# Cross-attention on one core: where two attention products of batch 30 and the first sums for x of batch 1 stand

## The chip, the cores and the metric

The kernel runs on one core of one Trainium2 chip. The core has TensorE (PE: matrix products out of SBUF into PSUM; PEld is its weight load), VectorE (DVE), ScalarE (ACT), GpSimd (POOL) and SyncE (SP, which only issues transfers here). GpSimd issues transfers too, and only those that add what they carry to what lies at their target. The metric is the time of one execution on the device in microseconds (us), median of three runs.

## What is computed

For each of 32 batches, x and y (the context) are 256 x 1024, f32. `w_qk`, `w_v` and `w_t` are 256 x 256.

```python
x_q = jnp.einsum('oc,bcn->bno', w_qk, y)
x_k = jnp.einsum('oc,bcn->bon', w_qk, x)
x_v = jnp.einsum('oc,bcn->bon', w_v, x) + b_v[None, :, None]
energy = jnp.einsum('bnc,bcm->bnm', x_q, x_k)
attention = jax.nn.softmax(energy, axis=-1)
attention = attention / (1e-07 + attention.sum(axis=1, keepdims=True))
x_r = jnp.einsum('bcn,bnm->bcm', x_v, attention)
x_r = jax.nn.relu(jnp.einsum('oc,bcn->bon', w_t, x - x_r) + b_t[None, :, None])
return x + x_r
```

The softmax runs along the rows; then each column is divided by its sum S over the rows. S needs the whole matrix of a batch, so nothing of the last product of a batch can start on the attention before S is there.

## The kernel before

**Seven products.** All is f32. Each large product is done as a 2 x 2 block product with seven block products instead of eight (Strassen's scheme in Winograd's form). They are called P1 to P7 here. The class `Seven` (L245) has what all four kinds share: three banks of PSUM, `one`, `two` and `three`; P1, P6, P7 and P4 follow one another in `one`, P5 and P3 in `two`, P2 in `three`. Between them ScalarE copies `one` after P1 (p1s), `two` after P5 (p5s) and `one` after P6 (w) into SBUF. VectorE makes a result block from one bank and one copy: c11 from P2 and p1s, c12 from P3 and w, c22 from P7 and p5s; c21 is P4's bank itself. P4 may only start in `one` when c22 has read it.

**The four kinds, per batch b.** `Keys` (pg) multiplies x by w_qk's square, result gx. `Values` (pu) makes ut from x, with w_t and w_v taken together. `Energy` (pe) makes the energies; a batch is cut into four tiles t = 0 to 3, called E0 to E3, each of which gives 128 rows of both halves of e; ScalarE takes the exp, and VectorE adds each row block, divided by its row sum, into `acc` (`share`, the "acc" rows). `Attention` (po) makes the output. `columns` (L543) reduces acc to `part`, `inverse` (L551) has a small product pS and turns it into rc, the inverse column sums, laid over all partitions.

**Attention.** A product has one call on x (`xpart`, L461, the x-call) and four on e (`epart`, L466, the e-calls, one for each block of 128 rows); a call is two MATMUL records[...]. `begin` issues the x-calls of P1, P5 and P2, which need no S. `run` (L505) has VectorE scale e by the row and column factors (`normal`, four instructions of 128x512 each time) and make t1 to t4 (`mix`, two instructions each): t1, t2 and t4 lie in a tile `et`, t3 in place of e's block b12 (L445). P1 needs normal(0,0), P2 normal(1,0), P5 t1, P6 t2, P3 b22, P7 t3, P4 t4. TensorE's order there is P1, P2, P5, P6's and P3's x-calls, half of P3's e-calls, P6, the rest of P3, P7. `combine` (L485) is two instructions on VectorE, the difference z and then relu plus x (L489), followed by the store. `end` (P4) and `c21` (relu on ScalarE, plus x on VectorE, the store) of batch b stand in batch b + 1, after P1 and P5 of its E0 (L612). In the last batch they stand at the very end.

**What overlaps S.** While VectorE and ScalarE finish E3 and S, TensorE has Keys and Values of the next batch to do. In the last batch there is no next one: after E3's P4 it has only `begin` (L682), then pS and then the attention of that batch.

**Sums.** The seven-product scheme needs sums of the blocks of each operand. For Values' result ut they are `us`, four subtractions on GpSimd (L365), in a pool with one buffer; us is read by P3, P5, P6 and P7 of the attention. For x and y of later batches (`summed`, L218) SyncE loads blocks into xs (ys), and three adding transfers by GpSimd, each of which needs the one before to have landed, complete them: `steps` at L238. For x these are `xsteps`, called at the ends of the tiles t = 1 to 3 (L647). Keys of the next batch needs xs: P5 the first of them, P6 the second, P4 the third. ut gets its bias by another such transfer, `u.bias()`, from uc.

**Order.** TensorE, VectorE, ScalarE and GpSimd each run their instructions in the order of the program text (`InOrder`, L66, ties each to the one before), so the text is the schedule of each engine; the recorded line of all of them is L77, and one goes by the names of tiles. Transfers by SyncE are in order on its queue. Waits between engines, and the choice of the buffer in a pool, are made by the framework. The pool `up` (x's sums, ut) and the pool `cp` of temporaries (p1s, p5s, w, z) have two buffers for each name, `one` and `et` one, PSUM eight banks.

Before the first batch, the text has Keys for batch 0, gt (the sums of Keys' result, L582), Values for batch 0 and `u.bias()`; E0 to E3 follow.

Of the kernel before, what the change touches and what calls it, by code (L numbers as in the profile page):

```python
# [9 lines left out]
F32 = mybir.dt.float32  # L10
AF = mybir.ActivationFunctionType
ALU = mybir.AluOpType
# [4 lines left out]
def kernel(  # L17
# [29 lines left out]
    nc = tc.nc  # L47
    B, C, N = x.shape
    P = 128
    KC = C // P  # L50
    NT = N // P
    MB = 512
    MH = N // MB
    HT = NT // 2
# [27 lines left out]
    pe, dve, act, pool = (InOrder(g) for g in (nc.tensor, nc.vector, nc.scalar, nc.gpsimd))  # L82
# [4 lines left out]
    loaded = {}  # L87

    def load(tag, b, pieces=1):
        from_, p = (x, xp) if tag == "x" else (y, yp)  # L90
        to = p.tile([P, KC, N], F32, tag=tag, name=f"{tag}_{b}")
        from_ = from_[b].rearrange("(k p) n -> p k n", p=P)
        W = KC // pieces
        for j in range(pieces):
            nc.sync.dma_start(to[:, ts(j, W)], from_[:, ts(j, W)])
        loaded[tag, b] = to
# [28 lines left out]
    bt = const.tile([P, KC, 1], F32, name="bt")  # L125
# [81 lines left out]
    up = ctx.enter_context(tc.tile_pool(name="up", bufs=2))  # L207
    one = ctx.enter_context(tc.tile_pool(name="one", bufs=1))
# [3 lines left out]
    def temp(tag, name):  # L212
        return cp.tile([P, MB], F32, tag=tag, name=name)
# [117 lines left out]
    class Values(Seven):  # L331
# [32 lines left out]

        def factors(self):  # L365

            us = one.tile([P, 4, HT, P], F32, tag="us", name=f"us_{self.b}")
            s1, s2, s3, s4 = (us[:, j] for j in range(4))
            a11, a12, a21, a22 = (self.block(i, h) for i in range(2) for h in range(2))
            steps = [  # L370
                lambda: pool.tensor_tensor(s1, a21, a22, ALU.add),
                lambda: pool.tensor_tensor(s2, s1, a11, ALU.subtract),
                lambda: pool.tensor_tensor(s3, a11, a21, ALU.subtract),
                lambda: pool.tensor_tensor(s4, a12, s2, ALU.subtract),
            ]
            return (a11, a12, s4, a22, s1, s2, s3), steps
# [58 lines left out]
    class Attention(Seven):  # L435


        def __init__(self, b, xr, ur):
            super().__init__("o", b)
            self.xr, self.ur = xr, ur  # L440
            et = ep.tile([P, 3, HT, MB], F32, tag="et", name=f"et_{b}")
            self.b11, self.b12 = e[:, :HT, ts(0, MB)], e[:, :HT, ts(1, MB)]
            self.b21, self.b22 = e[:, HT:, ts(0, MB)], e[:, HT:, ts(1, MB)]
            self.t1, self.t2, self.t4 = (et[:, j] for j in range(3))
            self.t3 = self.b12  # L445
            self.er = self.b11, self.b21, self.b22, self.t4, self.t1, self.t2, self.t3

        def normal(self, half, h):
# [14 lines left out]
                into, t_left[j - 1], self.xr[j - 1], start=not onto, stop=False, skip_group_check=True  # L463
            )

        def epart(self, into, j, tiles=range(HT)):  # L466
            for t in tiles:
                pe.matmul(
                    into,
                    self.ur[j - 1][:, t],  # L470
                    self.er[j - 1][:, t],
                    start=False,
                    stop=(t == HT - 1),
                    skip_group_check=True,
                )
# [9 lines left out]
        def combine(self, i, h, in0, in1, op):  # L485
            z = temp("z", f"z_{self.b}_{i}_{h}")
            dve.tensor_tensor(z, in0, in1, op)
            xt = loaded["x", self.b]
            dve.scalar_tensor_tensor(z, z, 0.0, xt[:, i, ts(h, MB)], ALU.max, ALU.add)  # L489
            self.store(i, h, z)  # L490
# [11 lines left out]
            self.xpart(self.two, 5)  # L502
            self.xpart(self.three, 2)

        def run(self, u):  # L505

            self.normal(0, 0)
            if u:
                u.c22()
            self.normal(1, 0)  # L510
            self.normal(0, 1)
            self.mix(self.t1, self.b11, self.b12, ALU.add)
            self.normal(1, 1)
            self.mix(self.t2, self.t1, self.b22, ALU.subtract)
            self.epart(self.one, 1)
            self.p1s = self.biased(self.one, "p1s", bt[:, 0, :])
            self.epart(self.three, 2)
            self.epart(self.two, 5)
            self.p5s = self.biased(self.two, "p5s", bt[:, 1, :])
            self.xpart(self.one, 6, True)  # L520
            if u:
                u.p4()
                u.c21()
                u.c11()
                u.c12()
            self.c11()
            self.xpart(self.two, 3, True)
            self.epart(self.two, 3, range(HT // 2))
            self.epart(self.one, 6)
            self.w = self.biased(self.one, "w", nbt[:, 0, :])  # L530
            self.mix(self.t3, self.b12, self.b22, ALU.subtract)
            self.mix(self.t4, self.b21, self.t2, ALU.subtract)
            self.epart(self.two, 3, range(HT // 2, HT))
            self.c12()
            self.xpart(self.one, 7, True)
            self.epart(self.one, 7)
            self.c22()

        def end(self):
            self.xpart(self.one, 4, True)  # L540
            self.epart(self.one, 4)

    def columns(b):  # L543

# [20 lines left out]
    xr, _ = summed("x", 0)  # L565
# [15 lines left out]
    lhs, gsteps = g.factors()  # L581
    for step in gsteps:  # L582
        step()
    u = Values(0, xr)
    u.p1()
    u.p5()
# [7 lines left out]
    u.p4()  # L594
    u.c21()
    u.bias()

    before = None
    for b in range(B):
        more = b + 1 < B  # L600
        pair = []

        for t in range(HT):
            now = Energy(b, t, lhs, rhs)
            pair.append(now)
            now.p1()
            if t > 0:
                pair[t - 1].exp(1)
            now.p5()
            if t == 0:  # L610
                if before is not None:
                    before.end()  # L612
                    before.c21()
                    if more:
                        load("x", b + 1)
                e = ep.tile([P, NT, N], F32, tag="e", name=f"e_{b}")
                acc = one.tile([P, N], F32, tag="acc", name=f"acc_{b}")
                ur, usteps = u.factors()
            if t > 1:
                pair[t - 2].share(0)  # L620
            if t == 0:
                now.p6()
            now.p2()
            now.c11()
            if t == 1:
                pair[0].scale(1)
            if t > 1:
                pair[t - 1].share(1)
            if t > 0:
                now.p6()  # L630
            if t == 1:
                act.activation(acc, e[:, HT, :], AF.Copy, scale=scales[HT])
            if t > 0:
                pair[t - 1].p4()
                pair[t - 1].c21()
                pair[t - 1].exp(0)
            now.p3()
            now.c12()
            now.p7()
            now.c22()  # L640
            if t == 0:
                for step in usteps:
                    step()
                if more:
                    xn, xsteps = summed("x", b + 1)
            elif more:
                xsteps[t - 1]()  # L647
        last = pair[-1]

        if more:  # L650
            g = Keys(b + 1, xn)
            g.p1()
        last.exp(1)
        if more:
            g.p5()
        pair[2].share(0)
        last.p4()
        last.c21()
        last.share(1)
        if more:  # L660
            load("y", b + 1)
            rhs, ysteps = summed("y", b + 1)
            g.p6()
        last.exp(0)
        if more:
            g.p2()
            g.c11()
            g.p3()
        last.share(0)
        part = columns(b)  # L670
        if more:
            g.p7()
            g.c12()
            g.c22()
            un = Values(b + 1, xn)
            un.p1()
            un.p5()
            un.p2()
            un.p6()
        else:  # L680
            now = Attention(b, xr, ur)
            now.begin()  # L682
        rc = inverse(b, part)
        if more:
            un.p3()
            g.p4()
            g.c21()
            un.p7()
            lhs, gsteps = g.factors()

        if more:
            now = Attention(b, xr, ur)
            now.begin()
            ysteps[0]()
            now.run(un)
            ysteps[1]()
            un.bias()
            for step in gsteps:
                step()
            ysteps[2]()  # L700
            before = now
            xr, u = xn, un
        else:
            now.run(None)
            now.end()
            now.c21()


# [28 lines left out]
```

## Time and profile before

| | us |
|---|---|
| median of 3 runs (2168.8 to 2169.19) | 2169.16 |
| the profiled execution | 2169.38 |
| its span, from first to last instruction | 2167.6 |
| TensorE busy | 2147.3 |
| VectorE busy | 1806.0 |
| ScalarE busy | 787.7 |
| GpSimd busy | 597.3 |
| mean granted clock of TensorE | 0.997 |

A row of the timeline has the start in us from the span's start, the busy time, the engine, the line, the operation, what is written from what, the shapes and the number of instructions merged; in brackets the idle time before it and what ended that. "SPq", "POOLq" are the issue of transfers. A row of the list of waits has who waited for whom: us in total, times, longest. A group's or a merged row's busy time holds overlapping records: MATMULs of 128x512 are recorded with 0.59 us each but start 0.43 us apart. What counts for the time is idle time of TensorE, which is busy for 99% of the span; batches start 66.56 us apart.

### The profile page before, as it was taken

Reading aid. Unit: us, or ns where it says so; the run is one execution under the profiler, and the core shown is the slowest. Engines: PE = TensorE matmul, PEld = TensorE weight load, DVE = VectorE, ACT = ScalarE, POOL = GpSimd, SP = SyncE. Lnnn points to the kernel's source line nnn. Section 1 sums busy time; section 2 is a strip of 40 time slices with the busy share of each in tenths; the row PEclk is TensorE's granted clock in tenths of the full one; section 3 lists DMA queues with packets and bytes.
Section 4 is the critical chain, followed back from the end, with each engine's and each line's share of the span. In section 5 each row is a group of like instructions: output and inputs, shape, how many; then the busy total and the mean of one; then the engine's idle time right before and its main releaser. Section 6 shows DMA issues by size and latency. Waiting matters only on the chain.

```text
span 2167.6 us, 19880 instructions
## 1 busy us (share of the span) xinstructions
PE 2147.3 (99%) x6366; PEld 1064.3 (49%) x6366; DVE 1806.0 (83%) x2963; ACT 787.7 (36%) x1321; POOL 597.3 (28%) x488
## 2 busy tenths in 40 slices
PE   9999999999999999999999999999999999999997
PEld 4455545554455545455544555444554545555453
DVE  5798888988888988889888888888898888988887
ACT  4134432344422444323443324443234433344421
POOL 4322323222233222332232322223322323223220
PEclk9999999999999999999999999999999999999999
DMA  5555666556655566565566554665555666556630
GB/s 142 123 121 140 146 130 146 114 125 155 153 124 126 120 148 146 122 144 115 135 150 140 133 124 122 149 154 121 132 118 143 146 128 149 111 128 155 144 75 20
DMA packets 139049, 282.60 MB, mean 130 GB/s; under 512 B 9152, under 2 KB 42688, under 8 KB 138944
## 3 DMA queue, kind: packets, MB, share of 16 engines
q0 software_dynamic: 75936, 114.83, 33.8%
q1 hardware_dynamic: 62464, 166.48, 23.0%
q8 instruction: 51, 0.84, 0.2%
q14 instruction: 54, 0.44, 0.1%
q10 hardware_dynamic: 544, 0.00, 0.0%
HBM read 181.67 MB, written 33.55 MB: 99 GB/s over the span
## 4 chain that ended last, share of the span: by engine, by line
PE 98%; DMA 1%; DVE 1%; issue 0%; POOL 0%; ACT 0%; DVEq 0%
PE po L77 44%; PE pe L77 34%; PE pu L77 9%; PE pg L77 9%; DMA xs<-xs 0%; DMA ut<-uc 0%; DMA xs<-in_x_dram 0%; PE idle L142 0%; DVE acc L77 0%; PE pS L77 0%; POOL us L77 0%; DVE e L77 0%; PE pw L184 0%; PE pg L169 0%; DVE z L77 0%
## 5 line engine op out<-in xcount | busy, mean ns | idle before, releaser
L77 PE MATMUL pe<-gt,ys 128*128 128x512 f32 x768 | 392.3, 592 | 0.0
L77 DVE SCALAR_TENSOR_TENSOR e<-e,ri,rc 128x512 f32<-128x512 f32 x512 | 348.4, 743 | 1.1
L77 DVE SCALAR_TENSOR_TENSOR acc<-e,ri,acc 128x1024 f32<-128x1024 f32 x224 | 289.0, 1290 | 8.0
L77 PE MATMUL pe<-gx,y 128*128 128x512 f32 x512 | 261.5, 592 | 0.0
L77 PEld LDWEIGHTS pe<-gt,ys 128*128 128x128 f32 x768 | 145.8, 190 | 184.1 <-issue 183.0
L77 PE MATMUL po<-e,us 128*128 128x512 f32 x512 | 235.4, 592 | 0.0
L77 PE MATMUL po<-e,ut 128*128 128x512 f32 x512 | 227.7, 598 | 2.7 <-DVE e L77 2.7
L77 PE MATMUL po<-et,us 128*128 128x512 f32 x512 | 230.2, 592 | 0.0
L77 POOL TENSOR_TENSOR gt<-gx 128x512 f32<-128x512 f32 x64 | 101.8, 1590 | 415.6 <-DVE gx L77 415.6
L77 ACT COPY ep1s<-pe 128x512 f32<-128x512 f32 x128 | 74.9, 585 | 306.1 <-PE pe L77 289.4
L77 ACT ACTIVATE e<-e,nm 128x1024 f32<-128x1024 f32 x128 | 147.1, 1149 | 99.1 <-DVE nm L77 97.6
L77 DVE TENSOR_TENSOR e<-e 128x1024 f32<-128x1024 f32 x64 | 178.9, 2833 | 0.0
L77 PEld LDWEIGHTS po<-e,ut 128*128 128x128 f32 x512 | 98.2, 192 | 126.5 <-issue 97.3
L77 PEld LDWEIGHTS po<-e,us 128*128 128x128 f32 x512 | 97.3, 190 | 122.4 <-issue 114.8
L77 PEld LDWEIGHTS pe<-gx,y 128*128 128x128 f32 x512 | 97.2, 190 | 121.9 <-issue 114.1
L77 PEld LDWEIGHTS po<-et,us 128*128 128x128 f32 x512 | 95.7, 190 | 124.1 <-issue 123.8
L77 DVE CUSTOM_DVE_ANT_0 e<-pe,ep1s 128x512 f32<-128x512 f32 x128 | 88.5, 691 | 79.6 <-ACT e L77 64.1
L77 DVE TENSOR_TENSOR z<-z,x 128x512 f32<-128x512 f32 x32 | 22.1, 692 | 153.9 <-ACT z L77 153.9
L77 ACT ACTIVATE e<-e,bias 128x1024 f32<-128x1024 f32 x128 | 147.4, 1152 | 0.5 <-DVE ri L77 0.5
L77 POOL DMA_DIRECT2D ut<-uc x32 | 50.7, 1584 | 313.1 <-DVE ut L77 257.2
L77 PE MATMUL pe<-gx,ys 128*128 128x512 f32 x256 | 130.9, 593 | 1.2 <-DVE nm L77 1.0
L77 PE MATMUL pe<-gt,y 128*128 128x512 f32 x256 | 130.7, 592 | 0.0
(113 smaller groups left out, 3360.9 us busy)
## 6 DMA issues: line engine op xcount, KB each, us to landing
y<-in_ctx_dram SPq DMA_DIRECT2D x32, 1024.0 KB, 4.9
ut<-uc POOLq DMA_DIRECT2D x32, 1024.0 KB, 9.7
out_dram<-z SPq DMA_DIRECT2D x128, 256.0 KB, 2.1
x<-in_x_dram SPq DMA_DIRECT2D x31, 1024.0 KB, 6.3
xs<-in_x_dram SPq DMA_DIRECT2D x62, 512.0 KB, 4.7
ys<-in_ctx_dram SPq DMA_DIRECT2D x62, 512.0 KB, 4.2
xs<-in_x_dram POOLq DMA_DIRECT2D x31, 512.0 KB, 9.2
xs<-xs POOLq DMA_DIRECT2D x31, 512.0 KB, 5.0
```

Source lines behind the costliest of these rows:

```text
L77: self.last = getattr(self.engine, name)(*args, **kwargs)
```

## The change

Six things are changed.

1. `us` comes from the pool with two buffers.
2. t3 goes into t1's place in `et` instead of e's block b12, so that P7 reads no part of e.
3. `combine` is split: `put` has the relu, the addition of x and the store. In all batches but the last two, P7, c22 and its `put` follow right behind `run`, where they stood at its end; c12 is in `run` for all but the last batch.
4. Of batch 30, P7 and P4 are left out where they stood, and take place in batch 31: P7's x-call before E3's P4, its e-calls behind E3's P4 and before `begin`, c22 behind `columns`, P4 behind pS; `put` and c21 stand in `run`, behind normal(1,0).
5. The end of the last batch is a function of its own, `finish`: P7 stands before the last e-call of P3, c22 before c12, and P4 with its relu, addition and store goes in two halves of 256 columns.
6. The sums for x of batch 1: the tile, its loads and the first adding transfer stand before Values of batch 0, the second and third behind `u.bias()`, and so ahead of the four us subtractions on GpSimd.

```diff
-            us = one.tile([P, 4, HT, P], F32, tag="us", name=f"us_{self.b}")
+            us = up.tile([P, 4, HT, P], F32, tag="us", name=f"us_{self.b}")
...
-            self.t3 = self.b12
+            self.t3 = self.t1
...
     def combine(self, i, h, in0, in1, op):
             z = temp("z", f"z_{self.b}_{i}_{h}")
             dve.tensor_tensor(z, in0, in1, op)
+            self.left = i, h, z
+
+        def put(self):
+            i, h, z = self.left
             xt = loaded["x", self.b]
             dve.scalar_tensor_tensor(z, z, 0.0, xt[:, i, ts(h, MB)], ALU.max, ALU.add)
             self.store(i, h, z)
...
-        def run(self, u):
+        def run(self, u, before=None):
...
             self.normal(1, 0)
+            if before:
+                before.put()
+                before.c21()
             self.normal(0, 1)
...
             self.c11()
+            self.put()
             self.xpart(self.two, 3, True)
-            self.epart(self.two, 3, range(HT // 2))
+            self.epart(self.two, 3, (0, 1))
             self.epart(self.one, 6)
...
-            self.epart(self.two, 3, range(HT // 2, HT))
-            self.c12()
-            self.xpart(self.one, 7, True)
-            self.epart(self.one, 7)
-            self.c22()
+            self.epart(self.two, 3, (2,))
+            if u:
+                self.epart(self.two, 3, (3,))
+                self.c12()
+                self.put()
...
+        def finish(self):
+            self.xpart(self.one, 7, True)
+            self.epart(self.one, 7)
+            self.epart(self.two, 3, (3,))
+            self.c22()
+            self.put()
+            self.c12()
+            self.put()
+            self.xpart(self.one, 4, True)
+            z = temp("z", f"z_{self.b}_1_0")
+            for cols in (ts(0, MB // 2), ts(1, MB // 2)):
+                self.epart(self.one, 4, cols=cols)
+                act.activation(
+                    z[:, cols], self.one[:, cols], AF.Relu, bias=bt[:, 1, :], scale=1.0
+                )
+                dve.tensor_tensor(
+                    z[:, cols], z[:, cols], loaded["x", self.b][:, 1, cols], ALU.add
+                )
+                nc.sync.dma_start(out[self.b, ts(1, P), cols], z[:, cols])
...
     for step in gsteps:
         step()
+    xn, xsteps = summed("x", 1)
+    xsteps[0]()
     u = Values(0, xr)
...
     u.bias()
+    xsteps[1]()
+    xsteps[2]()
...
             if t == 0:
-                if before is not None:
+                if before is not None and more:
                     before.end()
                     before.c21()
-                    if more:
-                        load("x", b + 1)
+                    load("x", b + 1)
...
-                if more:
+                if more and b > 0:
                     xn, xsteps = summed("x", b + 1)
-            elif more:
+            elif more and b > 0:
                 xsteps[t - 1]()
...
         last.exp(1)
         if more:
             g.p5()
+        else:
+            before.xpart(before.one, 7, True)
         pair[2].share(0)
         last.p4()
...
+        else:
+            before.epart(before.one, 7)
         last.exp(0)
...
+        else:
+            now = Attention(b, xr, ur)
+            now.begin()
         last.share(0)
         part = columns(b)
...
         else:
-            now = Attention(b, xr, ur)
-            now.begin()
+            before.c22()
         rc = inverse(b, part)
...
             now.run(un)
+            if b + 2 < B:
+                now.xpart(now.one, 7, True)
+                now.epart(now.one, 7)
+                now.c22()
+                now.put()
...
         else:
-            now.run(None)
-            now.end()
-            now.c21()
+            before.end()
+            now.run(None, before)
+            now.finish()
```

More of the change, by code (lines that the diff above doesn't have):

```diff
@@ L464, in xpart, with epart @@
             )
-        def epart(self, into, j, tiles=range(HT)):
+        def epart(self, into, j, tiles=range(HT), cols=slice(0, MB)):
             for t in tiles:
                 pe.matmul(
-                    into,
+                    into[:, cols],
                     self.ur[j - 1][:, t],
-                    self.er[j - 1][:, t],
+                    self.er[j - 1][:, t, cols],
                     start=False,
```

## The prediction

> **What bounds the kernel now.** I read the page's busy times first, then the list of waits for TensorE, then the timeline and the windows around each wait. The page:
>
> ```profile
> PE 2147.3 (99%) x6366; PEld 1064.3 (49%) x6366; DVE 1806.0 (83%) x2963; ACT 787.7 (36%) x1321; POOL 597.3 (28%) x488
> ```
>
> TensorE is the bound: only 20 us of the span are not busy. The list of waits says where its idle time is:
>
> ```profile
> PE pg L77 <- DMA xs<-xs: 5.7, 1, 5.7
> PE po L77 <- DVE e L77: 2.7, 1, 2.7
> PE pS L77 <- DVE part L77: 2.7, 1, 2.7
> ```
>
> Each occurs once in 32 batches, so the steady loop (66.56 us a batch in the chain of waits) has nothing to give. The 5.7 is in batch 0, the two 2.7 in batch 31. The timeline of batch 0:
>
> ```profile
> 26.87 1.72 POOL L77 DMA_DIRECT2D ut<-uc  x1 [4.47 <-ACT ut L77]
> ...
> 42.06 1.19 POOL L77 DMA_DIRECT2D xs<-in_x_dram  x1
> 48.21 1.20 POOL L77 DMA_DIRECT2D xs<-xs  x1 [4.95 <-DMA xs<-in_x_dram]
> ...
> 51.21 1.13 PE L77 MATMUL pe<-gx,ys 128*128 128x512 f32 x2
> ...
> 58.01 2.05 PE L77 MATMUL pg<-xs,gs 128*128 128x512 f32 x2 [5.68 <-DMA xs<-xs]
> 59.85 1.75 PE L77 MATMUL pg<-x,g 128*128 128x512 f32 x2
> 61.44 1.02 PE L77 MATMUL pg<-x,gs 128*128 128x512 f32 x2
> ```
>
> GpSimd stands idle from 22.41 to 26.87, then until 35.98 for ut's bias to land, makes the four us and only then starts x's sums for batch 1; the second lands at 57.87 where Keys' sixth product wants it at 52.17. A matmul call is two MATMULs, 0.857 us from start to start; the first two after the wait take 1.84 and 1.59. The windows (columns: us, busy PE, PEld, DVE, ACT, POOL, then granted clock) say why, and show the same in batch 31:
>
> ```profile
> 58.00:60.00 2.00, 1.99 (x3) 0.97 (x4) 0.00 (x0) 0.00 (x0) 0.92 (x1) 0.50 0.71 222
> 2129.80:2136.60 6.80, 5.36 (x7) 2.27 (x8) 6.76 (x11) 0.00 (x0) 0.00 (x0) 0.50 0.00 0
> ```
>
> The timeline of that place in batch 31:
>
> ```profile
> 2121.71 1.12 PE L77 MATMUL pe<-gx,ys 128*128 128x512 f32 x2 [1.05 <-DVE nm L77]
> ...
> 2128.09 0.41 PE L77 MATMUL pS<-part,fold 128*128 128x32 f32 x2 [2.68 <-DVE part L77]
> ...
> 2131.24 9.79 PE L77 MATMUL po<-e,ut 128*128 128x512 f32 x16 [2.74 <-DVE e L77]
> ```
>
> Idle for 1.05, 2.68 and 2.74 us, then at half clock until 2136.6.
>
> **The head.** Three transfers by GpSimd move. The first sum is issued right after gt, at 22.5 instead of 42.06; its loads by SyncE landed at 17.39 and keep their place. With 5.9 us as now it lands at 28.4. The bias keeps its issue at 26.87, as it waits for ut. The second sum waits for the first and the bias' issue (28.59): issued at 28.7, with its worst duration now (9.7) it lands at 38.4; were it to run wholly behind the bias (9.0), at 47. Needed at 52.17: hidden either way. The third (4.3 us) follows by 43 to 51, needed near 60. The us subtractions are now behind the third sum's issue: 40 to 45, at worst 48 to 53; their reader is attention of batch 0, after 64. So the wait of 58.01 - 52.17 = 5.84 goes, and with it the half clock: four MATMULs took 3.43 instead of 1.71, another 1.72. Sum 7.56.
>
> What is late next is VectorE. A us subtraction beside an acc sum costs it 1.1 us:
>
> ```profile
> 40.83 2.38 DVE L77 SCALAR_TENSOR_TENSOR acc<-e,ri,acc 128x1024 f32<-128x1024 f32 x1
> ```
>
> (the usual acc is 1.29). In batch 1, TensorE's last energy product has 0.5 us to spare for VectorE, in batch 0 it waits 0.29 (50.92 to 51.21). I take one such collision again, since us stays in that stretch; VectorE's lag then costs a further 0.2 at attention's fifth product, which has 0.25 to spare in batch 1. None would give +0.3, two -1.1. **Head: -7.35 (-6.2 to -7.85).**
>
> Here a rule weighs against the change: the Trainium skill, DMA: Bandwidth & Descriptors, "Anatomy of one DMA", gives a GpSimd transfer as about 2.0 us + bytes / 436 GB/s; an estimate from it is 3.2 us for these 512 KB, so that both would have landed by 49 and nothing waited: the head worth 0. The rows say 5.9 and 9.7, and TensorE did wait; I go by the rows.
>
> **The steady loop.** The order of TensorE and VectorE is the same (c22 and its put stand after run instead of at its end). t3 goes to t1's place, which the fifth product has long read (sum t3 is more than 4 us behind it): 0. us has a second buffer, so GpSimd need not wait for the seventh product:
>
> ```profile
> 163.05 1.26 POOL L77 TENSOR_TENSOR us<-ut 128x512 f32<-128x512 f32 x1 [4.92 <-PE po L77]
> ...
> 164.51 1.02 PE L77 MATMUL po<-xs,wtT 128*128 128x512 f32 x2
> ```
>
> But ut is issued at 153.17 and takes 9.7: the start can move by 0.2 at most. 0.
>
> **The last batch.** P7 and P4 of batch 30, 5 calls each, leave its start: 10 x 0.857 = 8.57. E0's sixth product loses the cover that P4 gave ScalarE's copy: 0.2, as in batch 0, where nothing stands between. The energies start 8.37 earlier if VectorE follows: at E0's c11 it still does c12 and put of batch 30 to 2093.3, where TensorE is ready near 2092.4; but it no longer does c22, its put and c21 there, and is 0.4 late at E0's c22 and level at E1. The last y sum lands at 2094.4, its reader moves from 2104.6 to 2096.2. us is done at 2098.9, the first acc on VectorE moves from 2109.83 to 2101.5: no collision. The kept p5s leaves one buffer of two, but ScalarE's next copy already stands behind the exp that waits for the same c22; the kept bank leaves 7, two energies use 6. Cost 0, at worst the 0.9 of one product in each of three tiles.
>
> From here in the old clock. P7's x-call fills 0.86 of the 1.05; its four e-calls follow the last energy product, from 2122.67, then the three of begin, to 2128.67. So pS, now queued behind them, comes 0.58 later, and the first normal at 2131.01. P4 covers that wait, 2128.95 to 2133.24. Attention's first two products run warm to 2140.1 (now 2140.86), their normals ready. The fifth waits: VectorE does 8 normals (5.31), put and c21's add (0.66 each), 4 normals (2.65), half of mix t1 (1.22), to 2141.5: a new wait of 1.47. Then 2141.57 + 3.43 = 2145.0; x-calls of 6 and 3 to 2146.8; P3's first half 2148.5; P6 2151.94; P3's third tile 2152.8; P7 2157.14; P3's fourth 2158.0, which covers c22; P4 from 2158.09: x-call 0.86, two halves of 1.73 (the 128x256 MATMULs at the start take 0.216) to 2162.57, now 2162.86. After that the relu is 0.4 instead of 0.7 and so the add (estimates: 0.38 is the row of a 128x256 ACTIVATE): 0.65 less; landing 2.0 and closing 1.24 stay. Another store costs SyncE 0.33, off the path. **Tail: -(8.37 + 0.29 + 0.65) = -9.3.** If the new wait were for all of t1, 1.1 less gain; but in batch 1 the fifth product starts after the first half.
>
> The second rule: the Trainium skill, TensorE: Matmul & The Clock Gate, "The HAM clock gate", halves the clock after an idle window of about 3.4 us. By it neither 2.68 nor 2.74 would do so, and 1.47 neither; the window above grants 0.50 all the same, since only 0.41 of work lay between the two. By the rule P1 would be warm already and some 2.6 us less is to be gained; I go by the row. The new wait of 1.47 stands alone, like the 1.05, after which the clock stayed 1.00.
>
> **Sum.** The profiled execution took 2169.38 (span 2167.6 and 1.8 around it), 0.2 above the median 2169.16. -7.35 - 9.3 = -16.65: **2152.5**, 0.77% faster. Within 0.2% (4.3 us) a measurement of this kernel can't tell it from no change.
>
> **Rivals.**
> Both gains as above: 0.77; 2150.5 to 2155.5 by the bounds given.
> VectorE becomes the bound of the last batch (it is busy without a gap from 2117, and gets two more steps before t1), or a kept buffer makes a wait: half of the 8.37 is lost, 2156.7; against it, its own chain also starts earlier. 0.09.
> The sums for x collide with the bias and the first loads, and the wait in batch 0 stays in part: up to all of 7.35 back, 2156 to 2160; against it, 5 us to spare in the worst order. 0.07.
> Slower: us, free of P7, starts early in every batch, and its subtractions hold up mix t4 and c12's put (two collisions, 2.2), so that c22 (163.00 to 163.69 in batch 1) is late for P4 (164.51), which has 0.8 to spare: 1.4 in each of 30 batches, 2152.5 + 42 = 2194. It decides from 0.55 a batch (16.65/30), so from 1.35 of delay, which wants ut to land some 2 us earlier than 9.7 after its issue; against it, it lands 0.2 before us starts in all batches. 0.05.
> The postponed products or the transfers don't land where the code puts them: no change, 2169. 0.02.
>
> The slower case is left out above and the deepest part of the others: **2150 to 2159**. Faster 0.93, same 0.02, slower 0.05.
>
> **What would show it.** Right: TensorE's waits list has no xs any more, and batch 0's half-clock window is gone; the two 2.7 waits become one near 1.5 before a po product fed by et; granted clock 1.00 throughout; the batch period stays 66.56. Wrong: a period above 66.6, us starting well before P7's end, a PE wait for an x sum, or VectorE ending waits in the last batch's energies.

## The result and the profile after

The changed kernel took 2153.48 us (median of 6 runs, 2152.95 to 2153.93) against 2169.24 (6 runs, 2168.8 to 2169.92): a ratio of 0.9927, 95% interval 0.9914 to 0.9940, 15.8 us less. The forecast was 2152.5. The profiled execution took 2153.93 with a span of 2152.1.

The page's busy times, and the list of waits for TensorE (us in total, times, longest; the two at the start, ahead of the first product, are left out):

```profile
PE 2143.6 (100%) x6374; PEld 1064.0 (49%) x6374; DVE 1803.4 (84%) x2964; ACT 788.5 (37%) x1322; POOL 597.4 (28%) x488
```

```profile
PE po L77 <- DVE et L77: 1.2, 1, 1.2
PE pu L77 <- DVE ut L77: 0.8, 1, 0.8
PE po L77 <- ACT z L77: 0.6, 1, 0.6
PE pe L77 <- DVE nm L77: 0.4, 2, 0.2
```

The three waits of 5.7, 2.7 and 2.7 are gone, and so is a smaller one of the kernel before, of the last P4 for c22:

```profile
PE po L77 <- DVE z L77: 0.8, 1, 0.8
```

The new order in `finish` covers that one; this order was not run alone. Two new waits stand in the last batch: 1.2 for t1 (forecast as 1.47) and 0.6 for a relu on ScalarE, which was not forecast.

Batch 0 on GpSimd and TensorE, from the timeline:

```profile
22.48 1.33 POOL L77 DMA_DIRECT2D xs<-in_x_dram  x1
27.03 1.58 POOL L77 DMA_DIRECT2D ut<-uc  x1 [3.22 <-ACT ut L77]
28.73 1.19 POOL L77 DMA_DIRECT2D xs<-xs  x1
39.13 0.92 POOL L77 DMA_DIRECT2D xs<-in_x_dram  x1 [9.21 <-DMA xs<-xs]
39.74 1.61 POOL L77 TENSOR_TENSOR us<-ut 128x512 f32<-128x512 f32 x1
...
51.37 1.12 PE L77 MATMUL pe<-gx,ys 128*128 128x512 f32 x2 [0.17 <-DVE nm L77]
52.33 1.02 PE L77 MATMUL pg<-xs,gs 128*128 128x512 f32 x2
```

The second sum for x landed at 38.84, and the product that needs it, Keys' sixth, starts at 52.33: without a wait, and the next call follows 0.86 later.

The last batch on TensorE (E0 starts at 2081.58):

```profile
2106.11 1.13 PE L77 MATMUL pe<-gx,ys 128*128 128x512 f32 x2 [0.19 <-DVE nm L77]
2107.08 3.60 PE L77 MATMUL po<-et,us 128*128 128x512 f32 x8
...
2113.09 0.30 PE L77 MATMUL pS<-part,fold 128*128 128x32 f32 x2
2113.23 1.10 PE L77 MATMUL po<-xs,wtT 128*128 128x512 f32 x2
2114.17 3.60 PE L77 MATMUL po<-et,ut 128*128 128x512 f32 x8
2117.60 7.03 PE L77 MATMUL po<-e,ut 128*128 128x512 f32 x16
2125.85 3.67 PE L77 MATMUL po<-et,us 128*128 128x512 f32 x8 [1.22 <-DVE et L77]
...
2143.77 1.89 PE L77 MATMUL po<-et,ut 128*128 128x256 f32 x8
2146.22 1.99 PE L77 MATMUL po<-et,ut 128*128 128x256 f32 x8 [0.56 <-ACT z L77]
```

P7 and P4 of batch 30 fill the stretch up to 2117.60; the attention's first sixteen MATMULs take 7.03 instead of 9.79. The windows (us, busy PE, PEld, DVE, ACT, POOL, granted clock, DMA share, GB/s) have full clock in both places:

```profile
51.00:56.00 5.00, 4.83 (x14) 2.24 (x14) 4.86 (x12) 4.04 (x9) 0.00 (x0) 1.00 0.93 351
2112.00:2125.80 13.80, 12.63 (x31) 5.35 (x29) 13.29 (x21) 1.37 (x2) 0.00 (x0) 1.00 0.11 39
```

Executions differ at the very start. TensorE begins each with six matmuls of zeros, which start at least 0.85 us apart until the clock is full and 0.43 apart after that; this comes sooner in some executions than in others, so that the first product of Keys' weights starts between 5.8 and 6.74 us after the start of the span in these traces (its weights have landed by 4.8 in all of them), and E0 of batch 0 between 24.85 and 26.22. So two executions can lie 1.4 us apart before E0 has begun, and stretches of traces are compared from marks inside them: A, from the first energy product of batch 0 to that of batch 1; B, from there to the first energy product of batch 31; C, from there to the end of the span.

| | A | B | C | A + B + C |
|---|---|---|---|---|
| before | 70.47 | 1996.79 | 74.58 | 2141.84 |
| after | 63.14 | 1992.50 | 70.57 | 2126.21 |
| difference | -7.33 | -4.29 | -4.01 | -15.63 |

B loses the 4.29 us of P7, which stood at its end; its other batches start 66.56 us apart in both.

### The profile page after: what moved, and what is told of

It is laid out like the page before. It is cut to its first block, busy times and chain, and to the rows that moved or that the text cites. A ratio compares the mean times of both kernels' runs of the same rounds, so it can differ in the third digit from the quotient of the medians.

```text
span 2152.1 us, 19871 instructions
## 1 busy us (share of the span) xinstructions
PE 2143.6 (100%) x6374; PEld 1064.0 (49%) x6374; DVE 1803.4 (84%) x2964; ACT 788.5 (37%) x1322; POOL 597.4 (28%) x488
## 4 chain that ended last, share of the span: by engine, by line
PE 98%; DVE 1%; issue 0%; ACT 0%; DVEq 0%
PE po L77 44%; PE pe L77 35%; PE pu L77 9%; PE pg L77 9%; DVE e L77 1%; PE idle L142 0%; DVE acc L77 0%; PE pS L77 0%; PE pw L184 0%; PE pg L169 0%; DVE z L77 0%; DVE rc L77 0%; DVE et L77 0%; ACT z L77 0%; PE pb L195 0%
## 5 line engine op out<-in xcount | busy, mean ns | idle before, releaser
L77 PE MATMUL po<-et,us 128*128 128x512 f32 x768 | 345.4, 592 | 1.2 <-DVE et L77 1.2
L77 DVE TENSOR_TENSOR et<-e 128x1024 f32<-128x1024 f32 x128 | 254.0, 2022 | 0.0
L77 PEld LDWEIGHTS po<-et,us 128*128 128x128 f32 x768 | 144.3, 190 | 187.0 <-issue 186.1
L77 DVE TENSOR_TENSOR z<-z,x 128x512 f32<-128x512 f32 (+1 forms) x33 | 22.3, 676 | 149.7 <-ACT z L77 149.7
L77 POOL TENSOR_TENSOR us<-ut 128x512 f32<-128x512 f32 x64 | 82.6, 1291 | 149.1 <-DMA ut<-uc 149.1
L77 PE MATMUL po<-e,us 128*128 128x512 f32 x256 | 120.5, 592 | 0.0
```

The source lines that it names most:

```text
L77: self.last = getattr(self.engine, name)(*args, **kwargs)
```

## The experiments

The medians are compared with runs of the kernel before on the same chip. With the first mark at the same place, A, B and C of each run's trace say where a difference lies.

| run | median us | before us | ratio, 95% interval | A | B | C |
|---|---|---|---|---|---|---|
| sums alone | 2161.53 | 2169.03 | 0.9968 (0.9956 to 0.9980) | 63.16 | 1996.79 | 73.55 |
| all but the sums | 2161.35 | 2169.03 | 0.9965 (0.9952 to 0.9978) | 71.61 | 1992.51 | 70.55 |
| buffer and t3 alone | 2169.35 | 2169.03 | 1.0002 (0.9993 to 1.0011) | 70.41 | 1996.80 | 74.50 |
| waits filled | 2166.34 | 2169.03 | 0.9987 (0.9978 to 0.9996) | 68.83 | 1996.79 | 73.55 |
| changed kernel again | 2153.29 | 2169.28 | 0.9926 (0.9914 to 0.9939) | 63.14 | 1992.50 | 70.56 |
| put behind t2 | 2152.15 | 2169.28 | 0.9921 (0.9907 to 0.9934) | 63.14 | 1992.50 | 69.69 |
| P4 whole | 2153.89 | 2169.28 | 0.9928 (0.9916 to 0.9941) | 63.13 | 1992.51 | 70.54 |
| put behind t2, P4 whole | 2152.36 | 2169.28 | 0.9922 (0.9909 to 0.9934) | 63.11 | 1992.51 | 69.68 |
| P4 alone kept | 2157.32 | 2168.84 | 0.9944 (0.9928 to 0.9961) | 63.14 | 1996.79 | 70.17 |
| sums behind the bias | 2153.89 | 2168.84 | 0.9930 (0.9915 to 0.9945) | 63.64 | 1992.50 | 70.56 |
| put behind t1 | 2151.60 | 2169.53 | 0.9918 (0.9905 to 0.9932) | 63.14 | 1992.50 | 69.36 |
| put behind t1, P3 laid out anew | 2151.10 | 2169.53 | 0.9916 (0.9903 to 0.9930) | 63.15 | 1992.50 | 68.54 |

### The sums alone, and all but the sums

```diff
--- the kernel before, with the sums alone
         step()
+    xn, xsteps = summed("x", 1)
+    xsteps[0]()
     u = Values(0, xr)
...
     u.bias()
+    xsteps[1]()
+    xsteps[2]()
...
-                if more:
+                if more and b > 0:
                     xn, xsteps = summed("x", b + 1)
-            elif more:
+            elif more and b > 0:
                 xsteps[t - 1]()
```

> The kernel before with only the three sums for x of batch 1 moved ahead of us. My theory, that the wait in batch 0 and the half clock after it are worth 7.2 to 7.4 us and independent of the last batch: 2162.0, no wait of TensorE for xs, the two 2.7 us waits in batch 31 still there. Rival, that the loads of y and the accumulations only trade places: above 2165. Rival, that head and tail share a cause: the gain differs from the 7.2 by which batch 31 starts earlier in the changed kernel.

The second run is the changed kernel with these same lines undone.

> The changed kernel with the sums for x of batch 1 back at their old place. Theory: the last batch keeps its gain of 8.3 us as the traces give it, the 5.7 us wait for xs is back: 2160.8. If the two parts are additive, the gains of this run and of the one with the head alone sum to 15.6 to 15.8.

Measured: 2161.53 (-7.50) and 2161.35 (-7.68), 15.2 together, where the changed kernel has 15.8. By the traces, from A to C, they gain 8.34 and 7.17, together 15.51 against 15.63; the medians' 0.6 is within what single executions of one kernel differ by (1.4 and 1.5 us in these two runs). With the sums alone no wait for xs is left and A falls by 7.31, as in the changed kernel; with all but the sums C is that of the changed kernel and B has lost P7. The two gains are separate, and the rivals that let the transfers merely trade places, or tie head and tail together, fall.

Each of the two traces met the half clock differently from the kernel before, although the code there is the same. In the run without the sums, Keys behind the wait for xs (timeline, then the window):

```profile
56.90 2.05 PE L77 MATMUL pg<-xs,gs 128*128 128x512 f32 x2 [5.44 <-DMA xs<-xs]
58.74 1.92 PE L77 MATMUL pg<-x,g 128*128 128x512 f32 x2
60.45 1.91 PE L77 MATMUL pg<-x,gs 128*128 128x512 f32 x2
62.15 1.44 PE L77 MATMUL pg<-xs,gs 128*128 128x512 f32 x2
```

Four calls are slow there (6.53 us for what takes 3.43), where in the kernel before two were (3.43 for 1.71). In the run with the sums alone, attention's P1 and P2 of batch 31 took 8.52 instead of 9.62:

```profile
2124.38 8.56 PE L77 MATMUL po<-e,ut 128*128 128x512 f32 x16 [2.74 <-DVE e L77]
```

```profile
2123.80:2127.30 3.50, 2.92 (x4) 1.37 (x5) 3.50 (x6) 0.00 (x0) 0.00 (x0) 0.51 0.00 0
```

Half clock for some 3.4 us, where it was 6.8 in the kernel before. So one and the same wait cost 1.1 us more in one trace (A 71.61 against 70.47) and another 1.0 less in the other (C 73.55 against 74.58); in the sum the two nearly cancel.

### The second buffer for us, and t3 in t1's place

```diff
-            us = one.tile([P, 4, HT, P], F32, tag="us", name=f"us_{self.b}")
+            us = up.tile([P, 4, HT, P], F32, tag="us", name=f"us_{self.b}")
...
-            self.t3 = self.b12
+            self.t3 = self.t1
```

> The kernel before with only the second buffer for us and t3 in t1's place. Theory: the steady loop costs and gains nothing, 2169.2 within 0.5, period 66.56, us starting 0.1 to 0.2 us earlier. Rival (the slower case): us starts early enough to hold up VectorE's c22 in each batch, 2190 or more; half a microsecond a batch would give 2185.

Measured 2169.35 against 2169.03, ratio 1.0002 (0.9993 to 1.0011), batches 66.560 us apart. us is now released by ut's landing and not by TensorE, and starts 0.1 us earlier in most batches (0.14 instead of 0.25 us after the first energy product, as counted in the traces):

```profile
163.06 1.26 POOL L77 TENSOR_TENSOR us<-ut 128x512 f32<-128x512 f32 x1 [5.19 <-DMA ut<-uc]
```

The slower case of the prediction needed ut to land some 2 us earlier. It falls, and with it a cost of these two edits in the loop.

### The waits filled

```diff
+    def fill(n, name):
+        spare = bank(f"fill_{name}")
+        for _ in range(n):
+            pe.matmul(spare, zeros[:, :P], zeros, start=True, stop=True)
...
+            if b == 0:
+                fill(6, "head")
             g.p6()
...
             now.begin()
+            fill(3, "part")
         rc = inverse(b, part)
+        if not more:
+            fill(3, "rc")
```

> The kernel before with matmuls of zeros into a spare bank placed in the three waits: six calls (5.1 us) ahead of Keys' sixth product in batch 0, three (2.6 us) behind begin and three behind pS in batch 31. The waits themselves stay (what is waited for comes no earlier), only TensorE is kept busy. Theory, that the half clock behind the waits is a cost of its own: -1.7 in batch 0, and about -1.2 in batch 31, where P1 and P2 become 2.7 faster but P5 then waits for t1: 2166.3, granted clock 1.00. Rival, that only the waits count: 2169.2 or a little above.

Measured 2166.34, 2.7 less, with more work on TensorE and nothing else changed. A falls by 1.64, C by 1.03. The clock was 1.00 in both places:

```profile
51.00:63.00 12.00, 11.48 (x39) 5.89 (x40) 6.45 (x11) 4.14 (x8) 0.92 (x1) 1.00 0.81 221
2121.00:2137.00 16.00, 15.24 (x36) 6.13 (x34) 15.29 (x24) 2.16 (x5) 0.00 (x0) 1.00 0.00 1
```

```profile
2129.29 7.13 PE L77 MATMUL po<-e,ut 128*128 128x512 f32 x16
2137.80 3.67 PE L77 MATMUL po<-et,us 128*128 128x512 f32 x8 [1.38 <-DVE et L77]
```

What each wait cost beyond its own length is shown here by itself: 1.6 in batch 0. In batch 31, P1 and P2 lose 2.5 us at half clock, of which 1.4 was hidden: with full clock TensorE waits that long for t1. The rival, that only the waits count, falls.

### P4 of batch 30 alone kept for the wait

P7 and c22 of batch 30 go back to their old place; P4, and c21 behind normal(1,0), stay in batch 31.

```diff
-                before.put()
                 before.c21()
...
-        else:
-            before.xpart(before.one, 7, True)
         pair[2].share(0)
...
-        else:
-            before.epart(before.one, 7)
         last.exp(0)
...
-        else:
-            before.c22()
         rc = inverse(b, part)
...
-            if b + 2 < B:
+            if more:
                 now.xpart(now.one, 7, True)
```

> The changed kernel with batch 30's P7 and c22 back at their old place; only P4 is postponed. Theory with the half clock: the energies of batch 31 start 4.3 us later than in the changed kernel, TensorE idles 2.8 us ahead of pS and the P4 and P1 behind it run in part at half clock: 2159.3. Theory without it (an idle time of 2.8 us between busy stretches does not lower the clock): 2157.1, clock 1.00.

Measured 2157.32, 3.8 to 4.0 above the changed kernel (2153.48 and 2153.29). That is the time expected without a half clock, but the clock was halved all the same:

```profile
2116.96 0.64 PE L77 MATMUL pS<-part,fold 128*128 128x32 f32 x2 [2.68 <-DVE part L77]
2117.41 2.05 PE L77 MATMUL po<-xs,wtT 128*128 128x512 f32 x2
2119.26 4.09 PE L77 MATMUL po<-et,ut 128*128 128x512 f32 x8
```

```profile
2116.90:2120.20 3.30, 3.24 (x6) 1.69 (x7) 2.47 (x5) 0.00 (x0) 0.00 (x0) 0.50 0.00 0
```

From its start to that of P1, P4 takes 5.77 where 4.37 was needed in the changed kernel. That is 1.4 lost, and t1's wait, 1.2 in the changed kernel and no longer in the list, took up nearly all of it. So both theories were wrong in part: the half clock came, and cost the total next to nothing. What the run does settle: P7 in the wait is worth nearly its whole length, 4.29 in B, of which 0.40 is given back in C. And an idle time of 2.68 us alone, with TensorE busy before and after it, did halve the clock here; the prediction's reason, two such waits with 0.41 of work between them, was not needed.

### The new wait ahead of P5

Beside the next runs the changed kernel ran once more.

> The changed kernel once more, as the base for the three runs beside it: 2153.5.

It took 2153.29. Batch 30's put and c21 on VectorE moved from behind normal(1,0) to behind t2:

```diff
             self.normal(1, 0)
-            if before:
-                before.put()
-                before.c21()
...
             self.mix(self.t2, self.t1, self.b22, ALU.subtract)
+            if before:
+                before.put()
+                before.c21()
```

> The changed kernel with batch 30's put and c21 on VectorE moved from behind normal(1,0) to behind the sum t2. Theory, that the new wait of 1.22 us ahead of attention's fifth product is made by these two steps (1.3 us): the wait falls to under 0.2, 2152.3. Rival, that the wait is VectorE's later start (pS behind begin, 0.6): half of it stays, 2152.9.

Measured 2152.15, C 0.87 less. The wait for et is out of TensorE's list: it was made by these two steps, and not by the later pS. But not all of the 1.22 came out at the end; VectorE's timeline says why:

```profile
2133.89 0.69 DVE L77 TENSOR_TENSOR z<-po,op1s 128x512 f32<-128x512 f32 x1 [3.02 <-DMA out_dram<-z]
```

c11 of batch 31 wants a buffer of z whose store has only just been issued; t3 behind it comes late for P7, which loses 0.3. Placed behind t1, the stores are out in time:

```diff
             self.mix(self.t1, self.b11, self.b12, ALU.add)
+            if before:
+                before.put()
+                before.c21()
             self.normal(1, 1)
```

> The changed kernel with batch 30's put and c21 on VectorE behind the sum t1 of batch 31, between the two places tried: early enough that their stores have landed when c11 of batch 31 wants z's buffer again. Theory, that the later place lost 0.3 us by that wait (3.0 us on VectorE, t3 late for the seventh product): 1.2 less than the changed kernel from the start of batch 31 to the end instead of 0.9, 2152.0. Rival, that the sum t2 now comes too late for the sixth product: 2152.5 or more.

Measured 2151.60, C 1.21 less than in the changed kernel: the whole wait.

### P4 in halves or whole

```diff
-            z = temp("z", f"z_{self.b}_1_0")
-            for cols in (ts(0, MB // 2), ts(1, MB // 2)):
-                self.epart(self.one, 4, cols=cols)
-                act.activation(
...
+            self.epart(self.one, 4)
+            self.c21()
```

> The changed kernel with the last P4, its relu, addition and store in one piece again. Theory, that the halves lose more than they gain since the second half's matmuls wait for ScalarE's read of the first half in the same bank (0.56 idle, 0.7 in all): 2153.1, no wait of TensorE for ScalarE's z. Rival, my prediction's sum, that the halves save 0.65: 2154.1.

Measured 2153.89 beside 2153.29, but C is 70.54 beside 70.56, and A and B agree within 0.01 too: no difference, and neither expectation. (The two profiled executions differ by 0.84, all of it before E0 of batch 0.) With P4 whole, TensorE's wait for ScalarE's z is gone, and the last addition ends 6.01 us after P4's x-call has started (2142.66 in this trace), against 6.38 with the halves (from 2141.80 in the changed kernel's trace beside it):

```profile
2147.97 0.69 DVE L77 TENSOR_TENSOR z<-z,x 128x512 f32<-128x512 f32 x1 [3.32 <-ACT z L77]
```

But the store of 256 KB behind it lands 2.01 us after its issue, and the last one of 128 KB in 1.72. The halves end 0.85 later on TensorE (5.41 after the x-call's start, against 4.56), and get it back in the last step of ScalarE (0.2 shorter) and of VectorE (0.3) and in the store (0.3).

The same together with the put behind t2:

> Both of the last two changes together. Theory: the gains add, 2151.9. Rival: what is gained ahead of P5 is lost at P7 or P4, because t3 and t4 come no earlier: 2153.

Measured 2152.36, C 69.68 against 69.69 with the halves: again only the put counts, and the sum of two gains that I expected is missed, since one of them is none.

If the halves' fault is the wait for ScalarE, other work between them should keep their gain. P3's five calls of the last batch were laid out anew, on top of the put behind t1:

```diff
-            self.epart(self.two, 3, (0, 1))
+            self.epart(self.two, 3, (0, 1) if u else (0,))
             self.epart(self.one, 6)
...
-            self.epart(self.two, 3, (2,))
+            self.epart(self.two, 3, (2,) if u else (1,))
...
             self.epart(self.one, 7)
-            self.epart(self.two, 3, (3,))
+            self.epart(self.two, 3, (2,))
             self.c22()
             self.put()
-            self.c12()
-            self.put()
...
                 self.epart(self.one, 4, cols=cols)
+                if cols.start == 0:
+                    self.epart(self.two, 3, (3,))
...
                 nc.sync.dma_start(out[self.b, ts(1, P), cols], z[:, cols])
+                if cols.start == 0:
+                    self.c12()
+                    self.put()
```

> The same with P3's five calls laid out otherwise in the last batch: x and one e-call ahead of P6, one behind P6, one behind P7, and the fourth between the two halves of P4, where TensorE waits for ScalarE's read of the first half (0.7); c12 follows the first half's addition. Theory, that TensorE then has no wait left from P5 to the end: 0.6 to 0.7 less than the run beside it, 2151.3. Rival, that P6 waits for t2 as it lost a cover, or c12 on VectorE delays the last addition: no gain.

Measured 2151.10 beside 2151.60, C 0.82 less; TensorE has no wait from P5 to the end:

```profile
2140.65 1.89 PE L77 MATMUL po<-et,ut 128*128 128x256 f32 x8
2142.38 1.02 PE L77 MATMUL po<-e,us 128*128 128x512 f32 x2
2143.24 1.89 PE L77 MATMUL po<-et,ut 128*128 128x256 f32 x8
```

This is the fastest version: 0.9916 of the kernel before (0.9903 to 0.9930), some 2 us less than the changed kernel.

### The sums behind the bias

```diff
     xn, xsteps = summed("x", 1)
-    xsteps[0]()
     u = Values(0, xr)
...
     u.bias()
+    xsteps[0]()
     xsteps[1]()
```

> The changed kernel with the first sum for x issued behind ut's bias too, so that all three stand between the bias and us. Theory, that the changed kernel has time to spare there (the second sum landed at 38.8, needed at 52.3): the sums land about 6 us later, us ends near 52, still no wait of TensorE for xs: 2153.5 within 0.5, or up to 1.1 more where one more acc on VectorE meets us. Rival, that the place ahead of the bias is what brings the gain: 2156 or more.

Measured 2153.89; A is 63.64, 0.5 more. No wait for xs: the third sum is issued at 45.39, as the second has landed, 7 us ahead of its use. What the later place costs is on VectorE, since us now runs from 45.98 to 52.26 and meets two acc sums, and attention's fifth product of batch 0 waits for t1:

```profile
72.27 3.24 PE L77 MATMUL po<-et,us 128*128 128x512 f32 x7 [0.90 <-DVE et L77]
```

So the gain of the head comes from standing ahead of us, not ahead of the bias.

## Why the prediction was right

**The head: forecast -7.35, measured -7.33.** The wait for xs and the half clock behind it went, as the sum had it. The first sum landed 5.96 us after its issue (5.9 was taken), the second 10.11 (9.7 was taken, 38.4 forecast, 38.84 measured). One collision of us with an acc sum was taken as 1.1; there were two, of together 1.1:

```profile
41.00 1.44 DVE L77 SCALAR_TENSOR_TENSOR acc<-e,ri,acc 128x1024 f32<-128x1024 f32 x1
...
44.92 2.21 DVE L77 SCALAR_TENSOR_TENSOR acc<-e,ri,acc 128x1024 f32<-128x1024 f32 x1
```

Going by the rows and not by the estimate of 3.2 us was right for this case: the second sum's 512 KB took 9.66 us before and 10.11 after.

**The steady loop: forecast 0, measured 0** (66.560 in both; 1.0002 with its two edits alone).

**The last batch: forecast -9.3, measured -8.30** (B and C). Its marks, from the start of E0, against the forecast's own times: the last energy product 24.53 (forecast 24.60), the first e-call of P5 44.27 (44.46), P4's x-call 61.23 (60.98), TensorE's end 66.63 (65.46). So the 8.37 by which the energies were to move, P7 and P4 under the waits, pS behind begin and the wait ahead of P5 (1.22 for 1.47) all came as worked out, each within 0.3. The half clock did stand behind the two waits of 2.7, as the row said and against the rule set beside it: with these waits filled, P1 and P2 took 2.5 us less (2.6 by the prediction).

**The step that was mis-sized** is P4 in two halves of 1.73 and "0.65 less" behind it. It was worked out as if the second half followed the first at once. In the trace it waits until ScalarE's relu has read the first half, in the same bank: 2146.22 instead of 2145.49. From P4's x-call to the end the forecast's sum has 8.6 us; the kernel before has 9.31 and the changed one 9.34. That is 0.8 of the 1.0 by which the last batch missed; the other 0.25 had gathered before P4's x-call. The halves bring nothing, as the run with P4 whole shows, and laid around another call they bring the 0.8. Whether two banks would have spared the wait was not tried.

The rivals are settled: VectorE does not become the bound of the energies (the last energy product waits 0.19 for it), the kept buffers make no wait, the sums for x have time to spare even behind the bias, and us does not start early.

One term was right by luck: the half clock's 1.72 in batch 0 is what the profiled execution of the kernel before had. The trace of all but the sums, where the same wait stands, had 3.1.

## What to carry to other kernels

A wait of TensorE for which work can be found elsewhere in the program was worth its length plus what the half clock behind it took, so far as no other engine hid it; where no useful work is at hand, matmuls of zeros still won a part of that (2.7 us here, in two places). Before a product is cut so that its result can be drained in parts, see whether the second part has to wait for the drain of the first, as it did here for 0.56 us in one bank, and whether other work can go between. A step that is moved on an engine takes its buffers with it: the place behind t2 took away one wait and made another through the store that held z.

## What was not expected of the hardware

The half clock came in lengths of 3.4 or 6.8 us. For the same idle times of 2.68 and 2.74 us around pS it was 6.8 us in the kernel before and 3.4 with the sums alone; an idle time of 2.68 us with TensorE busy on both sides was enough for 3.4 us.

What it goes with can be read from the traces. In each of the 14, the granted clock changes only at whole multiples of 3.41 us from its first change, and this grid lies differently to the program in each execution. The windows, cut along the grid, are these for the stretch around pS and P1, first in the kernel before and then with the sums alone:

```profile
2126.37:2129.78 3.41, 0.41 (x2) 0.30 (x2) 2.81 (x5) 0.00 (x0) 0.00 (x0) 1.00 0.00 0
2129.78:2133.20 3.42, 1.96 (x3) 0.93 (x4) 3.38 (x6) 0.00 (x0) 0.00 (x0) 0.50 0.00 0
2133.20:2136.61 3.41, 3.41 (x6) 1.34 (x5) 3.41 (x6) 0.00 (x0) 0.00 (x0) 0.50 0.00 0
2136.61:2140.02 3.41, 3.41 (x10) 1.50 (x9) 3.41 (x5) 0.69 (x1) 0.00 (x0) 1.00 0.00 0
```

```profile
2117.05:2120.46 3.41, 1.50 (x4) 0.38 (x2) 3.30 (x5) 1.24 (x2) 0.00 (x0) 1.00 0.01 2
2120.46:2123.88 3.42, 0.41 (x2) 0.30 (x2) 2.82 (x5) 0.00 (x0) 0.00 (x0) 1.00 0.00 0
2123.88:2127.29 3.41, 2.91 (x4) 1.36 (x5) 3.41 (x6) 0.00 (x0) 0.00 (x0) 0.50 0.00 0
2127.29:2130.70 3.41, 3.41 (x10) 1.50 (x9) 3.41 (x6) 0.69 (x1) 0.00 (x0) 1.00 0.00 0
```

TensorE's busy time in one stretch goes with the clock of the next. At full clock, stretches with 1.36 us of work or less were followed by half clock (the 1.36 is in the trace of buffer and t3 alone), those with 1.50 or more were not. At half clock, 2.66 or less kept it (the 2.66 is in batch 0 of the trace of all but the sums), and 2.91 or more ended it. So the same wait costs one stretch or two, by where the grid falls: in batch 0 one of the two slow stretches lay wholly inside the wait for xs in the kernel before (1.7 us lost), and neither in the trace of all but the sums (3.1 us). One execution's half clock is thus no more than a sample.
